# Four stages of a Perceiver kernel: pool waits by tile, one engine for token quantizing, first products before the norm, a narrower band

## The chip, the cores and the metric

The kernel runs on one core of a Trainium2 chip. A core has TensorE (PE in the profile, with its weight loads as PEld), VectorE (DVE), ScalarE (ACT), GpSimd (POOL) and SyncE (SP), whose queue issues the transfers. The engines run side by side and wait for each other by semaphores. The metric is the device time of one execution in microseconds. The kernel before took 2548.41 us (median of 3 runs, 2545.22 to 2550.57).

## The reference

A Perceiver with four layers is applied to 2 x 256 latents of 256 features. Each layer is a cross attention to a context of 2 x 4096 tokens, a self attention and a feed-forward block; each block adds its output to the stream, and the stream is normalized without parameters ahead of most blocks. What the change touches:

```
def _layernorm(x, axis=-1, eps=1e-05):
    m = jnp.mean(x, axis=axis, keepdims=True)
    v = jnp.var(x, axis=axis, keepdims=True)
    return (x - m) / jnp.sqrt(v + eps)
# L0_ffn: activations to 8 bits per token, weights to three values
def act_quant(x):
    scale = 127.0 / jnp.clip(jnp.max(jnp.abs(x), axis=-1, keepdims=True), 1e-05)
    return jnp.clip(jnp.round(x * scale), -128, 127) / scale
def weight_quant(w):
    scale = 1.0 / jnp.clip(jnp.mean(jnp.abs(w)), 1e-05)
    return jnp.clip(jnp.round(w * scale), -1, 1) / scale
def bit_linear(x, w):
    xq = x + jax.lax.stop_gradient(act_quant(x) - x)
    wq = w + jax.lax.stop_gradient(weight_quant(w) - w)
    return jnp.einsum('bsd,hd->bsh', xq, wq)
```

L0_ffn is bit_linear to 1024 hidden features, a convolution over three neighbouring tokens, SiLU, and bit_linear back. L1_ffn is a mixture of 16 experts of 128 hidden features, of which the gate picks two per token by sigmoid scores, and a shared expert that every token uses. L3_attn is a self attention in which a token sees the tokens at most 128 away. L3_ffn is a small two-layer transformer of its own; each of its layers ends with a feed-forward block of 682 hidden features with GELU gating, behind a layer norm with scale and offset.

## The kernel before

The stream x is held transposed, as two tiles of 128 features by 512 tokens (d = 0, 1). Products are in fp32, a product of 128x128 by 128x512 being two PE instructions. The function perceiver runs eleven blocks in order: l0_xattn, l0_attn, l0_ffn_and_l1_xattn, l1_attn, l1_ffn, l2_xattn, l2_attn, l2_ffn, l3_xattn, l3_attn, l3_ffn.

*The norm.* center (L221) makes the mean by products with a constant matrix, subtracts it on DVE (L232) and, with gamma given, also multiplies by it; measure (L239) squares on ACT (L233), sums by 16 small products (var), and takes root and reciprocal per token (L249, L250, the tile rstd); widen and widened spread rstd over the partitions by products (rstd_ps) and a copy on ACT (L269). layernorm (L272) does all of it and multiplies (L281, L283, L287); norm is layernorm of x.

*Order.* Where a block does not say otherwise, the framework's scheduler orders the instructions of each engine by its own model, with the program's order as priority; `nc.any` leaves the engine of a copy to it. The context attentions, L1_attn and L3_attn are written under manual_schedule of PE, DVE and ACT, whose instructions then run in the program's order. L0_ffn has only PE by program.

*Pools.* Tiles in SBUF come from pools that open and close like a stack, so a block's pool lies on the memory of an earlier block's pools. By default the first tile of a new pool waits until the earlier pools on its memory are released whole; with reuse_waits="tile" each tile waits only for the earlier tiles that it overlaps. The pools of PSUM banks and of temporaries (banks and stage, L86 and L97) wait by tile already; the blocks' pools don't.

*L0_attn and L0_ffn.* l0_attn ends with quantizing the weights of the block after it (quantize_weights, L542): w1 on DVE, w2 on POOL, with scratch tiles quant from L0_attn's work pool. l0_ffn (L1236) turns the normed stream to tokens (to_tokens, tok_ps, into hn), quantizes each token's row (quantize_tokens, L528: a maximum, four small operations on the scale, then quantize, L517, with its five steps L522 to L526), turns it back (from_tokens, L568, feat_ps, into hq), multiplies by w1 (proj), applies the convolution and SiLU (hid), and does the same for the hidden features, one tile of 128 tokens after the other (by_token, hid_tok, tok, hidq), ending with w2 (l0f_out). The rounding is `round(t) = (t * scale + MAGIC) - MAGIC`, and L525 and L526 add the rounding difference to the value as the reference does. In by_token, L525 is given to POOL:

```
net.quantize_tokens(work, tok, tok, 1, nc.gpsimd)
```

Between its steps l0_ffn runs pieces of a generator (run(between, 1)): the first three key projections of layer 1's context attention (begin, L800; k_ps, k_dense). That attention's tiles are made ahead of l0_ffn (ContextAttention, L780), and its 14 key tiles are filled with ones on POOL (L792) before rows of keys and masks are copied into them by transfers.

*L1_ffn* (L1492) norms x, multiplies the normed h by the gate's weights (gate_ps), and then goes through the shared expert (e = -1) and the 16 experts: two products into a bank pair (expert), SiLU, times the second half, times the token's share, and down (moe_acc). The routing (value, top, one, weight, wT) runs on DVE meanwhile.

*L3_attn* is SmallAttention (L1320) with a window: 8 units of batch and head group. both (L1404) makes the scores of a unit, once with queries on the partitions (for the maxima) and once with keys there; before the scores of each bank it adds the band mask, a bf16 product with the identity over all 512 columns (L1410). The mask's tile is made on POOL (mask_tile, L1861) and cast on DVE (L1881).

*L3_ffn* (L1895): in the feed-forward part of each of the two layers, layernorm gives h2, and six groups m of hidden features follow (ffn_ps, GELU, hid), then ffn_out.

## Time and profile before

The profile is of one execution.

| | |
|---|---|
| profiled execution | 2544.49 us, its span 2542.8 |
| PE busy | 2326.5 us, 91% of the span |
| DVE, ACT, POOL busy | 1544.8, 1083.0, 352.1 us |
| mean granted PE clock | 0.957 |
| L0_xattn | 0 to 704 us |
| L0_attn | 704 to 847 |
| L0_ffn | 847 to 948 |
| L1_xattn | 948 to 1630 |
| L1_attn | 1630 to 1718 |
| L1_ffn | 1718 to 1830 |
| L2_xattn, L2_attn, L2_ffn | 1830 to 1965, to 2086, to 2112 |
| L3_xattn, L3_attn, L3_ffn | 2112 to 2167, to 2271, to 2542 |

How to read the lines: the chain of waits goes back from the last instruction, at each step to what released it; its lines give start, duration, engine, tile and line of code. A timeline gives what ran in a stretch, in order, whether it is on the chain or not. A line on stretches gives the length, then each engine's busy time with its count of instructions, then the PE clock granted (1.00 is full), the DMA engines' share and GB/s.

### The profile page before, as it was taken

What the parts mean: (1) busy time and instruction counts of PE and PEld (TensorE: products, weight loads), DVE (VectorE), ACT (ScalarE), POOL (GpSimd) and SP (SyncE); (2) the same over time, 40 slices, a digit from 0 to 9 for tenths busy, and PEclk for the clock granted to TensorE, in tenths of its full rate; (3) what the DMA queues carried; (4) which work ended last, traced back from release to release, by engine and by line L of the source; (5) the groups of instructions that cost most, each with busy time, mean ns of one, the idle gap of its engine ahead of it and who ended that gap; (6) DMA issues with size and microseconds to landing.
All of it is one profiled execution on the core that took longest, in us unless ns stands there. A gap on an engine that the chain in (4) does not pass through costs nothing.

```text
span 2542.8 us, 42543 instructions
## 1 busy us (share of the span) xinstructions
PE 2326.5 (91%) x17014; PEld 1237.4 (49%) x17014; DVE 1544.8 (61%) x2702; ACT 1083.0 (43%) x1898; POOL 352.1 (14%) x523
## 2 busy tenths in 40 slices
PE   7999999999998579999999999989999986889998
PEld 3454545544544354544454544554448443445453
DVE  5878887778546467887878878343332354335252
ACT  2456555565616133555555566431131352223141
POOL 3000010000034612000010000000020131003030
PEclk9999999999999789999999999988999997998988
DMA  5432222231010133222322220202222100000100
GB/s 194 141 97 85 89 89 89 72 109 43 10 56 16 48 108 108 93 93 91 101 93 86 75 78 26 82 14 62 87 89 90 42 18 14 34 21 12 57 12 21
DMA packets 97797, 174.40 MB, mean 69 GB/s; under 512 B 15120, under 2 KB 63888, under 8 KB 96704
## 3 DMA queue, kind: packets, MB, share of 16 engines
q1 hardware_dynamic: 97600, 171.68, 21.0%
q8 instruction: 135, 2.21, 0.4%
q14 instruction: 62, 0.51, 0.1%
HBM read 154.25 MB, written 0.59 MB: 61 GB/s over the span
## 4 chain that ended last, share of the span: by engine, by line
PE 80%; DVE 10%; ACT 5%; issue 2%; POOL 1%; DMA 1%; SPq 0%; ACTq 0%; DVEq 0%; POOLq 0%
PE s L1098 11%; PE s L1122 11%; PE attn_acc L1146 9%; PE v_ps L180 6%; PE proj L180 5%; PE k_ps L1019 4%; DVE mx L1106 3%; PE f_ps L180 3%; PE expert L180 2%; PE kc_sum L180 2%; PE s L180 2%; PE c_acc L1684 2%; PE ffn_ps L180 2%; PE s L1420 2%; PE o L411 1%
## 5 line engine op out<-in xcount | busy, mean ns | idle before, releaser
L1106 DVE TENSOR_REDUCE mx<-s 128x2 f32<-128x1024 f32 x512 | 603.2, 1221 | 219.1 <-PE s L1098 216.3
L1132 ACT ACTIVATE p<-s 128x1024 f32<-128x1024 f32 x512 | 496.1, 1021 | 253.0 <-PE s L1122 250.9
L1122 PE MATMUL s<-xa_q,xa_k 32*128 32x256 f32 x4096 | 341.3, 402 | 26.0 <-DVE mx L1106 23.0
L1098 PE MATMUL s<-xa_k,xa_q 32*128 32x512 f32 x2048 | 337.5, 641 | 6.2 <-issue 2.8
L1122 PEld LDWEIGHTS s<-xa_q,xa_k 32*128 32x128 f32 x4096 | 212.0, 184 | 167.4 <-issue 92.6
L1146 PE MATMUL attn_acc<-p,xv 128*32 128x256 f32 x4096 | 275.3, 385 | 0.7 <-ACT p L1132 0.7
L657 DVE TENSOR_TENSOR ge<-fy 128x960 bf16<-128x960 f32 (+14 forms) x240 | 169.6, 707 | 6.5
L1098 PEld LDWEIGHTS s<-xa_k,xa_q 32*128 32x128 f32 x2048 | 111.4, 183 | 123.1 <-issue 62.5
L1146 PEld LDWEIGHTS attn_acc<-p,xv 128*32 128x32 f32 x4096 | 107.2, 109 | 130.8 <-issue 83.6
L611 POOL TENSOR_TENSOR fy<-fy,low 128x256 f32<-128x256 f32 x64 | 46.4, 726 | 875.5 <-ACT fy L610 875.2
L659 DVE TENSOR_TENSOR rank<-rank,ge 128x960 bf16<-128x960 bf16 (+14 forms) x240 | 104.2, 434 | 6.0
L661 DVE TENSOR_TENSOR rank<-rank,ge 128x960 bf16<-128x960 bf16 (+14 forms) x240 | 100.9, 420 | 2.6
L387 POOL TENSOR_SCALAR p<-p,r 128x128 f32<-128x128 f32 (+1 forms) x192 | 83.1, 446 | 138.4 <-DVE r L383 79.0
L1066 ACT COPY xv<-v_ps 128x512 f32<-128x512 f32 x64 | 37.6, 588 | 135.7 <-PE v_ps L180 125.8
L368 ACT ACTIVATE p<-p,top 128x256 f32<-128x256 f32 (+1 forms) x128 | 57.1, 447 | 41.5 <-DVE top L356 37.2
L180 PE MATMUL f_ps<-f_wk,f_ctx 128*128 128x256 f32 x256 | 68.9, 400 | 0.0
L233 ACT ACTIVATE sq<-xc 128x512 f32<-128x512 f32 x24 | 14.7, 630 | 126.0 <-DVE xc L232 126.0
L1019 PE MATMUL k_ps<-ctx_k,w_L0x_wq 128*64 128x512 f32 x256 | 65.5, 607 | 2.4 <-DMA ctx_k<-in_ctxT 1.9
L180 PE MATMUL v_ps<-w_L0x_wv,ctx_v 128*128 128x256 f32 x256 | 65.6, 400 | 0.8 <-ACT k_dense L1032 0.8
L1684 PE MATMUL c_acc<-pT,ctx_n 128*128 128x256 f32 x256 | 62.2, 388 | 4.2 <-ACT pT L1657 3.0
L180 PEld LDWEIGHTS f_ps<-f_wk,f_ctx 128*128 128x128 f32 x256 | 44.4, 189 | 42.7 <-issue 27.3
L180 PE MATMUL kc_sum<-f_tok,fy 128*128 128x257 f32 x256 | 64.2, 393 | 0.0
(460 smaller groups left out, 3380.0 us busy)
## 6 DMA issues: line engine op xcount, KB each, us to landing
ctx_k<-in_ctxT SPq DMA_DIRECT2D x128, 512.0 KB
ctx_v<-in_ctxT SPq DMA_DIRECT2D x64, 256.0 KB
xa_k<-k_dense SPq DMA_DIRECT2D x512, 32.0 KB
f_ctx<-in_ctxT SPq DMA_DIRECT2D x32, 256.0 KB
f_tok<-in_ctx SPq DMA_DIRECT2D x16, 512.0 KB
ctxT<-in_ctxT SPq DMA_DIRECT2D x16, 512.0 KB
ctx_n<-in_ctx SPq DMA_DIRECT2D x16, 512.0 KB
xa_k<-key_masks SPq DMA_DIRECT2D x128, 8.0 KB
```

The costliest lines, as they stand in the source:

```text
L180: self.nc.tensor.matmul(out, lhsT=lhsT, rhs=rhs, start=i == 0, stop=i == len(pairs) - 1)
L387: nc.gpsimd.tensor_scalar(p[:, j, :nk], p[:, j, :nk], r[:, j : j + 1], 1.0, ALU.mult, ALU.mult)
L657: nc.vector.tensor_tensor(ge[:, :, :n], w[:, :, :n], w[:, :, P - n :], ALU.is_ge)
L659: nc.vector.tensor_tensor(rank[:, :, P - n :], rank[:, :, P - n :], ge[:, :, :n], ALU.add)
L661: nc.vector.tensor_tensor(rank[:, :, :n], rank[:, :, :n], ge[:, :, :n], ALU.subtract)
L1019: nc.tensor.matmul(ps[i * HR : (i + 1) * HR, :], lhsT=self.wk[:, d, c * HR : (c + 1) * HR], rhs=ctx[:, d, :], start=d == 0, stop=d == ND - 1,)
L1098: nc.tensor.matmul(pairs[i // 2][:, i % 2, :], lhsT=self.q[u][rows, qt * P : (qt + 1) * P], rhs=k[rows, :], start=True, stop=True,)
L1106: nc.vector.tensor_reduce(mx[:, qt, 2 * i : 2 * i + 2, kc], sc, AX.X, ALU.max)
L1122: nc.tensor.matmul(pairs[i // 2][:, i % 2, kk * S : (kk + 1) * S], lhsT=k[rows, at], rhs=self.q[u][rows, :], start=True, stop=True,)
L1132: nc.scalar.activation(p, sc, AF.Exp, scale=DH**-0.5)
L1146: nc.tensor.matmul(self.acc[i * HP : (i + 1) * HP, :S], lhsT=v[:, 2 * k2 + kk, at : at + HP], rhs=ps[i // 2][:, i % 2, kk * S : (kk + 1) * S],
L1684: nc.tensor.matmul(accs[m], lhsT=of[:, (k + i) % (KC // P), m * P : (m + 1) * P], rhs=pT[:, i, :], start=k + i == 0, stop=k + i == KT - 1,)
```

## The change

It has six parts. (1) All pools of the blocks are opened with reuse_waits="tile". (2) quantize runs all its steps on one engine, with four scratch tiles in place of two, and returns its scratch, which holds the rounding difference; in by_token the difference is subtracted on DVE and no longer added there: from_tokens accumulates two products with the identity, of the value and of the difference, where it had one transpose. (3) The 14 key tiles of layer 1 are filled on ACT from a tile of ones in begin, and run(between, 1) is called once more in l0_ffn to run that piece. (4) L1_ffn: the gate's and the shared expert's products take the centred stream; the gate's result is multiplied by rstd per token, the shared expert's two by the widened rstd, and h is made by two multiplications. (5) L3_ffn: the first two of six groups take the centred (and scaled) stream, are multiplied by the widened rstd, and get the offset's contribution through a bias made by small products. (6) In the function both of SmallAttention, the mask's product comes after the scores and covers columns 128 to 383 of 512 alone.

```diff
@@ -446,7 +446,7 @@
-        with tc.tile_pool(name="xa", bufs=1) as big, tc.tile_pool(name="xa_ctx", bufs=2) as cpool:
+        with tc.tile_pool(name="xa", bufs=1, reuse_waits="tile") as big, tc.tile_pool(name="xa_ctx", bufs=2, reuse_waits="tile") as cpool:
...
@@ -514,18 +514,20 @@
-    def quantize(self, work, out, src, scale, inverse, low, high, first, second, third):
+    def quantize(self, work, out, src, scale, inverse, low, high, engine):
...
-        t = work.tile([P, 1024], F32, tag="quant", name="quant", bufs=2)[:, :n]
-        first.tensor_scalar(t, src, scale, MAGIC, ALU.mult, ALU.add)
-        first.tensor_scalar(t, t, MAGIC, low, ALU.subtract, ALU.max)
-        first.tensor_scalar(t, t, high, inverse, ALU.min, ALU.mult)
-        second.tensor_tensor(t, t, src, ALU.subtract)
-        third.tensor_tensor(out, t, src, ALU.add)
-    def quantize_tokens(self, work, out, src, rows, between=None):
+        t = work.tile([P, 1024], F32, tag="quant", name="quant", bufs=4)[:, :n]
+        engine.tensor_scalar(t, src, scale, MAGIC, ALU.mult, ALU.add)
+        engine.tensor_scalar(t, t, MAGIC, low, ALU.subtract, ALU.max)
+        engine.tensor_scalar(t, t, high, inverse, ALU.min, ALU.mult)
+        engine.tensor_tensor(t, t, src, ALU.subtract)
+        if out is not None:
+            engine.tensor_tensor(out, t, src, ALU.add)
+        return t
+    def quantize_tokens(self, work, out, src, rows):
@@ -535,9 +537,12 @@
         nc.vector.reciprocal(inverse, scale)
+        more = []
         for r in range(rows):
             of = scale[:, r : r + 1], inverse[:, r : r + 1]
-            self.quantize(work, out[:, r, :], src[:, r, :], *of, -128.0, 127.0, nc.vector, between or nc.vector, nc.vector)
+            to = None if out is None else out[:, r, :]
+            more.append(self.quantize(work, to, src[:, r, :], *of, -128.0, 127.0, nc.vector))
+        return more
@@ -565,13 +570,18 @@
-    def from_tokens(self, outs, src, n):
+    def from_tokens(self, outs, src, n, more=None):
...
             for i in range(k):
-                self.nc.tensor.transpose(ps[:, i * P : (i + 1) * P], src[:, (m + i) * P : (m + i + 1) * P], self.ident)
+                at, to = slice((m + i) * P, (m + i + 1) * P), ps[:, i * P : (i + 1) * P]
+                if more is None:
+                    self.nc.tensor.transpose(to, src[:, at], self.ident)
+                else:
+                    self.matmuls(to, [(of[:, at], self.ident) for of in (src, more)])
             self.copy(outs(m, k), ps[:, : k * P].rearrange("p (k t) -> p k t", k=k))
@@ -788,8 +798,9 @@
         self.key_tiles = [tile([P, KC], f"k{i}") for i in range(self.KEY_TILES)]
-        for t in self.key_tiles:
-            self.nc.gpsimd.memset(t, 1.0)
+        if layer == 0:
+            for t in self.key_tiles:
+                self.nc.gpsimd.memset(t, 1.0)
         self.begun, self.beginning = 0, iter(())
@@ -800,6 +811,10 @@
         self.begun = n
+        if self.layer > 0:
+            for t in self.key_tiles:
+                self.nc.scalar.copy(t, self.net.ones[:, 0:1].to_broadcast([P, KC]))
+            yield
         for j in range(n):
...
@@ -1239,11 +1254,12 @@
...
         h = net.norm(x)
...
         net.quantize_tokens(work, hn, hn, NT)
+        run(between, 1)
@@ -1274,15 +1290,15 @@
             nc.scalar.copy(tok[:, 0, :], sc.rearrange("p a b -> p (a b)"))
-            net.quantize_tokens(work, tok, tok, 1, nc.gpsimd)
-            toks.append(tok)
+            toks.append((tok[:, 0, :], *net.quantize_tokens(work, None, tok, 1)))
...
-            net.from_tokens(lambda m, k: hidq[:, m : m + k, at], toks[t][:, 0, :], NCH)
+            tok, more = toks[t]
+            net.from_tokens(lambda m, k: hidq[:, m : m + k, at], tok, NCH, more)
...
@@ -1404,16 +1421,9 @@
         nc = self.nc
         pairs = [self.net.sc(name) for _ in range(2)]
-        for i in range(NG if self.mask is not None else 0):
-            nc.tensor.matmul(
-                pairs[i // 2][:, i % 2, :],
-                lhsT=self.net.ident16,
-                rhs=self.mask.rearrange("p q k -> p (q k)"),
-                start=True,
-                stop=False,
-            )
         for half in range(2):
@@ -1421,9 +1431,17 @@
                     rhs=columns_of[rows, :],
-                    start=self.mask is None,
-                    stop=self.mask is None or half == 1,
+                    start=self.mask is None or half == 0,
+                    stop=self.mask is None,
                 )
+        for i in range(NG if self.mask is not None else 0):
+            nc.tensor.matmul(
+                pairs[i // 2][:, i % 2, P : P + S],
+                lhsT=self.net.ident16,
+                rhs=self.mask.rearrange("p q k -> p (q k)")[:, P : P + S],
+                start=False,
+                stop=True,
+            )
         return pairs
@@ -1496,34 +1514,54 @@
     nc.gpsimd.iota(number, pattern=[[1, E]], base=0, channel_multiplier=0, allow_small_or_imprecise_dtypes=True)
-    h = net.norm(x)
-    hc = [h[:, d, :] for d in range(ND)]
...
+    norm = net.center(net.halves(x))
...
         tile3 = lambda name: big.tile([P, NT, E], F32, name=name, tag=name)
...
         for t in range(NT):
-            net.matmuls(ps[:, t * E : (t + 1) * E], [(c[:, t * P : (t + 1) * P], gw[:, d, :]) for d, c in enumerate(hc)])
-        nc.vector.tensor_tensor(
-            value,
-            ps[:, : NT * E].rearrange("p (t e) -> p t e", t=NT),
-            gb.unsqueeze(1).to_broadcast([P, NT, E]),
-            ALU.add,
-        )
+            net.matmuls(
+                ps[:, t * E : (t + 1) * E], [(c[:, t * P : (t + 1) * P], gw[:, d, :]) for d, c in enumerate(norm.chunks)]
+            )
+        def hidden(wg, wu, of):
+            sc = net.sc("expert")
+            for n, w in enumerate((wg, wu)):
+                net.matmuls(sc[:, n, :], [(w[:, d, :], c) for d, c in enumerate(of)])
+            return sc
+        shared = hidden(sg, su, norm.chunks)
+        net.measure(norm)
+        for t in range(NT):
+            nc.vector.scalar_tensor_tensor(
+                value[:, t, :], ps[:, t * E : (t + 1) * E], norm.rstd[:, t : t + 1], gb, ALU.mult, ALU.add
+            )
         nc.scalar.activation(value, value, AF.Sigmoid)
+        factor = net.widened(norm.rstd)
+        a = work.tile([P, T], F32, tag="a", name="a", bufs=3)
+        first = work.tile([P, T], F32, tag="shared", name="shared", bufs=1)
+        nc.vector.tensor_tensor(a, shared[:, 0, :], factor, ALU.mult)
+        nc.vector.tensor_tensor(first, shared[:, 1, :], factor, ALU.mult)
+        nc.scalar.activation(a, a, AF.Silu)
+        nc.vector.tensor_tensor(first, first, a, ALU.mult)
+        h = big.tile([P, ND, T], F32, name="h", tag="h")
+        for d in range(ND):
+            nc.vector.tensor_tensor(h[:, d, :], norm.chunks[d], factor, ALU.mult)
+        hc = net.halves(h)
...
@@ -1556,19 +1594,15 @@
             if e < 0:
-                wg, wu, wd = sg, su, sd
-            elif e % 2 == 0:
-                pair = net.load(*(f"L1f_e{w}{e + i}" for i in range(2) for w in "gud"))
-                wg, wu, wd = pair[:3]
+                wd, a = sd, first
             else:
-                wg, wu, wd = pair[3:]
-            sc = net.sc("expert")
-            for n, w in enumerate((wg, wu)):
-                net.matmuls(sc[:, n, :], [(w[:, d, :], c) for d, c in enumerate(hc)])
-            a = work.tile([P, T], F32, tag="a", name="a", bufs=3)
-            nc.scalar.activation(a, sc[:, 0, :], AF.Silu)
-            nc.vector.tensor_tensor(a, a, sc[:, 1, :], ALU.mult)
-            if e >= 0:
+                if e % 2 == 0:
+                    pair = net.load(*(f"L1f_e{w}{e + i}" for i in range(2) for w in "gud"))
+                wg, wu, wd = pair[e % 2 * 3 : e % 2 * 3 + 3]
+                sc = hidden(wg, wu, hc)
+                a = work.tile([P, T], F32, tag="a", name="a", bufs=3)
+                nc.scalar.activation(a, sc[:, 0, :], AF.Silu)
+                nc.vector.tensor_tensor(a, a, sc[:, 1, :], ALU.mult)
                 share = net.mm("share")
...
@@ -1987,21 +2021,47 @@
-            h = net.layernorm([y[:, 0, :], shifted(net, work, y, 1, "shift_b")], "h2", gamma=lg, beta=lb)
-            hc = [h[:, d, :] for d in range(ND)]
+            norm = net.center([y[:, 0, :], shifted(net, work, y, 1, "shift_b")], gamma=lg)
             w2 = net.load(n("w2"))
             hid = big.tile([P, NHC, T], F32, name="hid", tag="hid")
-            for m in range(NHC):
+            def hidden(m, of):
                 k = min(P, HID - m * P)
-                at = slice(m * P, m * P + k)
                 sc = net.sc("ffn_ps")
                 for i, w in enumerate((w1a, w1g)):
-                    net.matmuls(sc[:k, i, :], [(w[:, d, at], c) for d, c in enumerate(hc)])
-                g = work.tile([P, T], F32, tag="gelu", name="gelu")
-                nc.scalar.activation(g[:k], sc[:k, 1, :], AF.Gelu, bias=b1[:k, 1, m : m + 1])
-                nc.vector.scalar_tensor_tensor(
-                    hid[:k, m, :], sc[:k, 0, :], b1[:k, 0, m : m + 1], g[:k], ALU.add, ALU.mult
-                )
+                    net.matmuls(sc[:k, i, :], [(w[:, d, m * P : m * P + k], c) for d, c in enumerate(of)])
+                return k, sc[:k, 0, :], sc[:k, 1, :]
+            def gated(m, k, a, g, bias):
+                t = work.tile([P, T], F32, tag="gelu", name="gelu")
+                nc.scalar.activation(t[:k], g, AF.Gelu, bias=bias[:k, 1, m : m + 1])
+                nc.vector.scalar_tensor_tensor(hid[:k, m, :], a, bias[:k, 0, m : m + 1], t[:k], ALU.add, ALU.mult)
+            made = [hidden(m, norm.chunks) for m in range(2)]
+            ps = net.mm("beta_ps")
+            for i, w in enumerate((w1a, w1g)):
+                for m in range(2):
+                    at = 2 * i + m
+                    net.matmuls(ps[:, at : at + 1], [(w[:, d, m * P : (m + 1) * P], lb[:, d : d + 1]) for d in range(ND)])
+            bias = big.tile([P, 2, 2], F32, name="bias", tag="bias")
+            nc.vector.tensor_tensor(bias, ps[:, :4].rearrange("p (i m) -> p i m", i=2), b1[:, :, :2], ALU.add)
+            net.measure(norm)
+            wide = net.widened(norm.rstd)
+            h = big.tile([P, ND, T], F32, name="h2", tag="h2")
+            for m, (k, a, g) in enumerate(made):
+                parts = [work.tile([P, T], F32, tag=f"by_token{i}", name=f"by_token{i}") for i in range(2)]
+                for of, part in ((g, parts[1]), (a, parts[0])):
+                    nc.vector.tensor_tensor(part, of, wide, ALU.mult)
+                if m == 0:
+                    for d in range(ND):
+                        nc.vector.tensor_tensor(h[:, d, :], norm.chunks[d], wide, ALU.mult)
+                        nc.vector.tensor_scalar_add(h[:, d, :], h[:, d, :], lb[:, d : d + 1])
+                gated(m, k, *parts, bias)
+            hc = net.halves(h)
+            for m in range(2, NHC):
+                gated(m, *hidden(m, hc), b1)
             new = net.new_x(big)
...
                 ps = net.mm("ffn_out")
```

## The prediction

> **What bounds the kernel now.** I read the page from its top down (engines, chain), then the chain of waits stage by stage for each place the diff touches, then the timeline around those places, then the stretches with their clock.
>
> ```profile
> PE 2326.5 (91%) x17014; PEld 1237.4 (49%) x17014; DVE 1544.8 (61%) x2702; ACT 1083.0 (43%) x1898; POOL 352.1 (14%) x523
> ...
> PE 80%; DVE 10%; ACT 5%; issue 2%; POOL 1%; DMA 1%; SPq 0%; ACTq 0%; DVEq 0%; POOLq 0%
> ```
>
> TensorE is busy 91% of the span and 80% of the chain. The two context attentions (0–704 and 948–1630 us) make up 54%, at clock 1.00, and the diff leaves their ordered loops alone. So the change can act only in the stages between, where the chain leaves PE. The first is the start of L0_ffn, in the chain of waits:
>
> ```profile
> 853.56 7.40 POOL quant L524 x2
> 860.96 4.60 POOL quant L525 x2
> ...
> 867.82 2.35 POOL w_L0f_w L526
> 870.19 0.70 DVE hn L219
> ...
> 870.99 1.23 DVE scale L533
> ...
> 872.24 4.78 DVE scale L534
> ```
>
> The copies into hn need tok_ps, which is complete at 859.07, and they wait until 870.19. What they wait for is GpSimd's quantizing of w2, whose scratch lies in a pool that the new pool replaces. Then a 128x4 operation (L534), 0.15 us elsewhere, takes 4.76; the timeline shows what runs beside it:
>
> ```profile
> 870.38 6.60 POOL L792 MEMSET xa_k<- 128x512 f32 x14
> ```
>
> It ends when these 14 fills end (877.0). Next the token stage of the same block, in the chain:
>
> ```profile
> 920.34 2.59 DVE quant L522
> ...
> 936.62 6.69 PE l0f_out L180 x32
> ...
> 944.42 3.84 PE l0f_out L180 x32
> ```
>
> Here DVE sets the pace (L522 takes 2.7 beside GpSimd's L525 and 0.74 alone), and one group of 32 products runs at half clock, 6.69 for 3.84. Last, one unit of L3_attn and the waist of the first L3_ffn layer, in the chain:
>
> ```profile
> 2228.38 0.59 PE sums L180 x4
> 2229.26 0.44 PE top_ps L1449 x2
> 2229.69 0.86 PE s L1410 x4
> 2230.56 1.08 PE s L1420 x16
> 2231.63 1.00 PE attn_acc L1467 x16
> 2232.63 0.97 PE s L1410 x4
> ...
> 2367.72 1.74 PE var L180 x14
> ...
> 2370.10 2.06 PE rstd_ps L180 x8
> ...
> 2372.18 1.41 DVE h L283 x2
> ...
> 2374.04 23.76 PE ffn_ps L180 x48
> ```
>
> The mask products (L1410) lie on PE's path, twice per unit of 7.58 us. In L3_ffn PE works little from 2365.69 (end of the mean) to 2374.04, and then starts 48 products at half clock. The stretches say where the clock is low:
>
> ```profile
> 853.90:888.00 34.10, 9.78 (x28) 6.09 (x29) 14.48 (x29) 1.71 (x4) 23.08 (x22) 0.50 0.11 36
> ...
> 1724.30:1737.90 13.60, 12.54 (x33) 8.11 (x34) 4.51 (x18) 2.84 (x4) 0.00 (x0) 0.50 0.00 1
> ...
> 2369.40:2379.60 10.20, 7.64 (x16) 4.24 (x16) 2.38 (x5) 1.55 (x2) 0.00 (x0) 0.50 0.01 2
> ```
>
> **The change part by part.** All sums are against the profiled execution, 2544.49 us (span 2542.8); the median of the runs, 2548.41, lies 3.9 above it.
>
> *Program start.* The fill of xa_top at 9.28 waits for the mask's transfer; key loads stand behind it on SP's queue and land at 14.96, where PE waits with k_ps. With a wait per tile the fill can go earlier. SP still issues in its old order, so I take 1.5 us; bounds 0 and 5 (nearly all of the 5.87 us transfer hidden).
>
> *L0_ffn's start.* hn overlaps oT and v of L0_attn, free at about 852, so by tile its copies start at about 859 and the reduce (1.23) ends at about 862. GpSimd's L525 and L526 of w2 then run back to back to 870.2. The nearest row, L534 held for 4.76 until the whole run of fills was over, says that DVE's small operation waits for the end of that run too: 870.2 in place of 877.0, a gain of 6.8. The 14 fills leave GpSimd for ScalarE: 14 x 0.59 (its 128x512 copy) = 8.3 us. ScalarE is idle 853.6–870.2 and is wanted next at about 873 (hq's copies came 3.8 after L535), so they hide; taken up only after 870.2, about 5.5 of them would stand before hq. SP's 14 key-mask loads only wait for these fills, and their readers come some 25 us later. I take 6.5; bounds 1 (those 5.5 show) and 16 (DVE gets between GpSimd's instructions).
>
> The Trainium skill, "SBUF — State Buffer", section "Who interferes with whom", says the loser is blocked until the other engine's instruction has finished. The row shows L534 blocked over about nine 0.525 us fills, so the run ended it, not one instruction. By the rule L534 would start at GpSimd's next boundary, about 863.3, and the whole sum would come out some 7 us lower.
>
> *Token stage.* Four times 2.35 of GpSimd's L525 goes, and DVE gets a 1.13 subtraction but loses the 1.13 addition (L526) and the 2 us of blocking: per tile 1.23 + 0.9 + 0.65 + 0.60 + 0.73 + 1.13 = 5.2 in place of 6.7. In exchange from_tokens issues 32 PE instructions per tile where it had 8 of 0.13: at 0.12 (l0f_out: 3.84/32) that is 3.84 in place of 1.06. So PE becomes the bound: 4 x (3.84 + 3.84) + 1.94 of k_ps = 32.7, from the first tile ready, 908.0 + 5.5 + 0.3 = 913.8, to 946.5, against 948.26. I take 2 us; bounds: a gain of 3 (the first tile isn't delayed by the next tile's reduce, 1.13), and a loss of 5 (two windows of half clock as at 915.3 and 935.8, each 6.8 us long and costing 3.4).
>
> *L1_ffn.* Before: mean ends 1720.27, first hidden product of an expert done at 1741.49. After: xc 0.7, gate at full clock 1.7, shared 8 x 0.43 = 3.44, var 1.74, rstd 0.5, rstd_ps 1.0, wide copy 0.6, then on DVE a, first and h, 4 x 0.69 = 2.8 with h's second half overlapped, then expert 0's 8 x 0.43 = 3.44: about 1735.9, 5.6 earlier. PE stands idle some 3 us before h. If that drops the clock, 3.44 doubles; a sigmoid table load of 1.28 ahead of the wide copy comes out of it as well. Cover for the routing (L1548's wT at 1744.06) is thinner: with experts 5.4 us earlier, wT could be late by 1 or 2. I take 4; bounds 2 and 6.5.
>
> *L3_ffn, twice.* From the mean's end to ffn_out, 32.1 now (2365.69–2397.80). After: centring with gamma 1.7, 16 products 6.9, beta 1.0, var 1.7, rstd 0.5, rstd_ps 0.95, copy 0.65, two parts 1.38, h 0.64 + 0.41 and 0.3 for its second half, 32 products 13.8 = 29.9, plus 0.3 of handovers: 1.9 less. PE idles 3.4 before h; at half clock for 6.8 us after it the layer loses 3.4, a net loss of 1.5. In the row above, half clock began after gaps of no more than 2 us, so I do not exclude it and take 1 us per layer, 2 in all; bounds −3 and +4 in all.
>
> The Trainium skill, "TensorE: Matmul & The Clock Gate", section "HAM oscillation — how this bites in real kernels", warns of PE gaps above about 3.4 us. The trace shows half clock after shorter ones. By the rule the new 3.4 us gap sits on the edge, and one lost window of about 3.4 us at half would cost 1.7 a layer and leave almost no gain.
>
> *L3_attn.* Its start: GpSimd's fills and affine selects for band_f end at 2170.5, and DVE's cast and xc stand behind them (2170.88), while the mean is done by 2169.5. By tile they go earlier: 1.5 us; bounds 0 and 3. Per unit, 8 mask products of 0.215 become 8 of about 0.107 (half the columns): −0.95 from 7.58. L1_attn's unit without mask takes 6.12; with 0.86 of mask 6.6 to 7.0. So 0.6 to 0.95 for each of five full units, and about 0.2 for each of the other groups, whose first masks already ran while DVE was reducing and now follow the scores. I take 4; bounds 2 and 6.
>
> Elsewhere (L0_attn, L1_attn, L2_xattn, L2_attn, L2_ffn) no wait for a pool stands on the chain, so waiting by tile is worth nothing there, give or take 3 for a different order of instructions.
>
> Sum: 1.5 + 6.5 + 2 + 4 + 2 + 1.5 + 4 = 21.5 us, so 2544.49 − 21.5 = 2523.0; against the median it would be 2526.9. I say 2524.
>
> **The rivals.**
>
> *PE idle and half clock eat the reordered parts.* For it: half clock follows today's short gaps in exactly these places, and the token stage has 11 us more PE work. Against it: the gaps are not longer in sum. Then the token stage loses 4, L1_ffn gains 2, L3_ffn loses 3, and the rest stands (1.5 + 6.5 + 1.5 + 4): 8.5 gained, 2536.
>
> *GpSimd gives DVE the port between instructions.* For it: at 965.98 L829 waited through one fill (1.31 in place of 0.41) with ten more to come. Against it: L534. L0_ffn's start gives 16 and not 6.5, which alone is 2513, and the parts that DVE leads gain with it: 2508.
>
> *Slower: early transfers get in front of the context's loads.* With waits by tile, loads and fills of the next block leave SP's queue as soon as single tiles are free, and SP issues in order: what waits there holds the ctx_k loads behind it. The chain of L0_xattn has one such stall already, 8.77 us on ctx_k at 67.56. Three more of that size in the two context attentions or L2_xattn (26.3) undo the sum of 21.5; from the fourth on (35.1) it decides: 2558. Against it: the DMA engines are at 0.3 of their time, and the attention's own order of loads is unchanged.
>
> *The change hardly acts:* hn overlaps the scratch that GpSimd uses or the copies are queued late, and only the bounds' low ends come: 2543 to 2550.
>
> **How the numbers follow.** Forecast case 0.57 (2513 to 2532); half clock 0.20 (2536); port 0.11 (2508); hardly acts 0.06; slower 0.06. A measurement of this kernel tells a change from none at about 0.2%, 5 us: 2543.3 to 2553.5 is the same. Faster is 0.57 + 0.20 + 0.11 = 0.88; same 0.06 (the case that hardly acts); slower 0.06. Best ends of all bounds together give about 2500, worst ends about 2550. For 8 in 10, leaving the slower case out: 2503 to 2546.
>
> **What would show it.** Right: hn's copies at about 859 and L535 near 870; no GpSimd work in the token stage, and 32-instruction feat_ps groups on the chain there; L1410 groups at half their time after the scores; gate_ps and expert ahead of var in L1_ffn, ffn_ps x16 ahead of var in L3_ffn. Wrong: hn still waiting for L526; half clock in the token stage or before h; longer DMA pieces in the chain of the context attentions.

## The result, and the profile after

The changed kernel takes 2542.59 us (median of 20 runs, 2535.51 to 2552.07) against 2547.39 (20 runs) for the kernel before. The ratio is 0.9984, 95% interval 0.9974 to 0.9993: about 4 us faster, where 21.5 were forecast. The time lies inside the range I gave, but the gain is a fifth of the one I worked out, and it is less than the 5 us (0.2%) below which I called two kernels the same.

The profiled execution of the changed kernel took 2547.81 us, 5.2 above its median, while the one of before was 2.9 below its own. So the two traces differ by +3.3 us (spans 2546.1 and 2542.8) where the medians differ by −4.8. Lengths of stages, from the first product of one block's mean to that of the next (L3_ffn in three pieces: its attention, the first feed-forward part with the second attention, the second feed-forward part), with the time at half clock in them:

| stage | before, us | half clock | after, us | half clock | forecast |
|---|---|---|---|---|---|
| L0_xattn (with the program's start) | 704.5 | 6.8 | 706.9 | 13.7 | −1.5 |
| L0_attn | 143.0 | 13.7 | 143.9 | 17.1 | 0 |
| L0_ffn | 100.5 | 47.8 | 92.4 | 30.7 | −8.5 |
| L1_xattn | 681.9 | 3.4 | 682.4 | 3.4 | 0 |
| L1_attn | 88.1 | 17.1 | 89.8 | 20.5 | 0 |
| L1_ffn | 111.3 | 13.7 | 111.0 | 13.7 | −4 |
| L2_xattn, L2_attn, L2_ffn | 283.3 | 20.4 | 280.3 | 17.0 | 0 |
| L3_xattn | 54.8 | 23.9 | 57.1 | 34.1 | 0 |
| L3_attn | 103.1 | 6.8 | 105.9 | 27.3 | −5.5 |
| L3_ffn, three pieces | 272.2 | 64.2 | 276.4 | 60.4 | −2 |

L0_ffn did what the forecast said. L3_attn, which should have lost 5.5 us, is 2.8 longer; L1_ffn stayed; L3_ffn grew. The page of the changed kernel, its engines and its chain:

```profile
PE 2346.3 (92%) x17142; PEld 1255.4 (49%) x17142; DVE 1544.8 (61%) x2719; ACT 1093.1 (43%) x1917; POOL 334.3 (13%) x505
...
PE 81%; DVE 9%; ACT 5%; issue 2%; POOL 1%; DMA 1%; SPq 0%; ACTq 0%; DVEq 0%; POOLq 0%
```

PE is busy 19.8 us more. At the start of L0_ffn, DVE's timeline (start, length, then what the engine had waited for):

```profile
861.89 0.69 DVE L219 COPY hn<-tok_ps 128x512 f32<-128x512 f32 x1 [1.00 <-PE tok_ps L568]
863.36 1.22 DVE L535 TENSOR_REDUCE scale<-hn 128x4 f32<-128x1024 f32 x1 [0.78 <-ACT hn L219]
864.61 1.86 DVE L536 TENSOR_SCALAR scale<-scale 128x4 f32<-128x4 f32 x1
866.50 0.18 DVE L537 RECIPROCAL scale<-scale 128x4 f32<-128x4 f32 x1
866.72 2.05 DVE L538 TENSOR_SCALAR scale<-scale 128x4 f32<-128x4 f32 x1
...
868.90 2.29 DVE L522 TENSOR_SCALAR quant<-hn,scale 128x256 f32<-128x256 f32 x1
873.48 0.40 DVE L522 TENSOR_SCALAR quant<-hn,scale 128x256 f32<-128x256 f32 x1 [2.29 <-POOL w_L0f_w L527]
```

hn waits for its transposes alone, as forecast. L536, L538 and L522 take about 2 us where 0.2 to 0.4 would do, beside GpSimd's L525 and L527, and a later L522 waits for the end of L527, because its scratch tile lies on one of w2's. The token stage, from the chain:

```profile
910.79 5.22 PE feat_ps L180 x30
916.01 3.68 PE l0f_out L180 x32
919.69 3.57 PE feat_ps L180 x32
923.27 3.62 PE l0f_out L180 x32
```

PE now goes from one group to the next without a wait. In L3_attn the chain shows the first units and then one of the steady units:

```profile
2200.84 2.02 PE s L1430 x16
2202.87 0.97 PE s L1438 x4
2203.83 2.97 PE s L1430 x16
...
2212.83 2.97 PE s L1430 x16
...
2229.61 0.59 PE sums L180 x4
...
2230.92 1.08 PE s L1430 x16
2232.00 0.54 PE s L1438 x4
...
2236.60 0.59 PE sums L180 x4
```

A steady unit takes 6.99 us, from one group of sums to the next (7.58 before). But in the first units a group of 16 scores takes 2 to 3 us for 1.08. And the first layer's feed-forward part in L3_ffn:

```profile
2363.61 0.86 PE mean L180 x2
2364.47 1.87 PE beta_ps L180 x16
2366.34 0.98 PE mean L180 x2
...
2369.13 7.08 PE ffn_ps L180 x16
2376.21 1.47 PE var L180 x14
...
2383.05 15.94 PE ffn_ps L180 x32
```

The products of the offset run between the two halves of the mean, and the 14 var products behind the 16 early ones. L1_ffn has the same order, 8 early products of the shared expert between the gate's and then var; the products of expert 0 wait for h until 1732.12:

```profile
1718.26 0.40 PE gate_ps L180 x2
1718.66 0.95 PE expert L180 x2
1719.61 1.47 PE gate_ps L180 x14
1721.08 4.37 PE expert L180 x6
1725.44 1.69 PE var L180 x16
...
1732.12 2.08 PE expert L180 x2
```

Stretches of the changed kernel at half clock (length, busy time of each engine, clock granted):

```profile
1728.00:1738.20 10.20, 7.60 (x15) 3.70 (x14) 8.50 (x36) 3.48 (x5) 0.52 (x1) 0.50 0.00 1
2199.00:2219.50 20.50, 18.87 (x103) 10.94 (x104) 7.01 (x8) 5.16 (x5) 0.00 (x0) 0.50 0.00 1
```

In the second one PE is busy 18.87 of 20.5 us, and still at half clock for 20 us on end. That is new in this block, which had 6.8 us at half clock in all before.

### The profile page after: what moved, and what is told of

Same layout as the page of the kernel before. It is cut to its first block, busy times and chain, and to the rows that moved or that the text cites. A ratio compares the mean times of both kernels' runs of the same rounds, so it can differ in the third digit from the quotient of the medians.

```text
span 2546.1 us, 42824 instructions
## 1 busy us (share of the span) xinstructions
PE 2346.3 (92%) x17142; PEld 1255.4 (49%) x17142; DVE 1544.8 (61%) x2719; ACT 1093.1 (43%) x1917; POOL 334.3 (13%) x505
## 4 chain that ended last, share of the span: by engine, by line
PE 81%; DVE 9%; ACT 5%; issue 2%; POOL 1%; DMA 1%; SPq 0%; ACTq 0%; DVEq 0%; POOLq 0%
PE s L1137 11%; PE s L1113 11%; PE attn_acc L1161 9%; PE v_ps L180 6%; PE proj L180 6%; PE k_ps L1034 5%; DVE mx L1121 3%; PE f_ps L180 2%; PE kc_sum L180 2%; PE expert L180 2%; PE s L180 2%; PE c_acc L1718 2%; PE ffn_ps L180 2%; PE s L1430 2%; PE o L411 1%
## 5 line engine op out<-in xcount | busy, mean ns | idle before, releaser
L1161 PE MATMUL attn_acc<-p,xv 128*32 128x256 f32 x4096 | 276.4, 386 | 0.7 <-ACT p L1147 0.7
L1113 PEld LDWEIGHTS s<-xa_k,xa_q 32*128 32x128 f32 x2048 | 111.3, 183 | 124.7 <-issue 60.1
L368 ACT ACTIVATE p<-p,top 128x256 f32<-128x256 f32 (+1 forms) x128 | 57.1, 447 | 65.5 <-DVE top L356 63.0
L180 PE MATMUL expert<-h,w_L1f_eg 128*128 128x512 f32 x128 | 61.8, 604 | 2.6 <-DVE h L1552 2.6
```

Source lines behind the costliest of these rows:

```text
L180: self.nc.tensor.matmul(out, lhsT=lhsT, rhs=rhs, start=i == 0, stop=i == len(pairs) - 1)
L1113: nc.tensor.matmul(pairs[i // 2][:, i % 2, :], lhsT=self.q[u][rows, qt * P : (qt + 1) * P], rhs=k[rows, :], start=True, stop=True,)
L1161: nc.tensor.matmul(self.acc[i * HP : (i + 1) * HP, :S], lhsT=v[:, 2 * k2 + kk, at : at + HP], rhs=ps[i // 2][:, i % 2, kk * S : (kk + 1) * S],
```

## The experiments

Theory A was: L0_ffn's gain is real; the mask products that L3_attn lost had kept PE's clock up; L3_ffn's reordering loses by itself. Its rival B: one unlucky profile. (Later theories and rivals have the letters C to G; each is given where it is tested.) Three kinds of kernels follow: parts alone and parts undone, repairs of the order, and PE's clock by itself. The kernel before was run beside each on the same chip; ratios are to it.

**The pools alone.** All `tile_pool(...)` of the blocks get the argument, nothing else:

```diff
-        with tc.tile_pool(name="xa", bufs=1) as big, tc.tile_pool(name="xa_ctx", bufs=2) as cpool:
+        with tc.tile_pool(name="xa", bufs=1, reuse_waits="tile") as big, tc.tile_pool(name="xa_ctx", bufs=2, reuse_waits="tile") as cpool:
```

> The kernel before with one part of the change alone: all block pools wait by tile. Theory A (the scratch of GpSimd's quantizing was what hn waited for, and the rest of L0_ffn's gain is the new quantizing): hn is copied near 862 as in the changed kernel, but the 14 fills stay on GpSimd behind w2 and keep holding DVE's small operations, so L0_ffn takes 96 to 99 us (100.5 before, 92.4 after), the other stages are unchanged at full clock, and the kernel is 2 to 4 us faster than before. Rival B (the pools carry all of it): L0_ffn takes 92 to 94 us and the kernel is 6 to 8 us faster.

Measured: 2550.98 us, ratio 1.0011 (0.9998 to 1.0024); L0_ffn 99.06 us. The stage is at the upper end of theory A, the whole is not there: the pools by themselves bring no time. DVE's timeline of this kernel shows why the early hn is worth only 1.5 us without the rest:

```profile
859.24 1.22 DVE L533 TENSOR_REDUCE scale<-hn 128x4 f32<-128x1024 f32 x1
860.50 0.23 DVE L534 TENSOR_SCALAR scale<-scale 128x4 f32<-128x4 f32 x1
...
867.76 9.28 DVE L522 TENSOR_SCALAR quant<-hn,scale 128x256 f32<-128x256 f32 x1 [2.31 <-POOL w_L0f_w L526]
```

L522 is held until 876.9, when the 14 fills (870.24, 6.65 us) are over. The wait for the pool goes, and the wait behind GpSimd's fills takes its place.

**The pools with the new quantizing and the fills on ScalarE.** The three other blocks as before:

```diff
-            net.quantize_tokens(work, tok, tok, 1, nc.gpsimd)
-            toks.append(tok)
+            toks.append((tok[:, 0, :], *net.quantize_tokens(work, None, tok, 1)))
...
+        if self.layer > 0:
+            for t in self.key_tiles:
+                self.nc.scalar.copy(t, self.net.ones[:, 0:1].to_broadcast([P, KC]))
+            yield
```

> The kernel before with the pools by tile, the new quantizing, the products in from_tokens and the fills on ScalarE; L1_ffn, L3_attn and L3_ffn as before. Theory A: L0_ffn 92 to 93 us, the rest as before, the whole 8 us faster than before (2539.5), that is 3 us faster than the whole change, because the other three parts together lose. Rival B: the other three parts gain on average and the profiled execution of the whole change was unlucky in its clock; then this kernel is 3 us or more slower than the whole change.

Measured: 2541.03 us, ratio 0.9980 (0.9965 to 0.9994); L0_ffn 90.92 us. So this part is worth about 5 us (1.5 to 9 by the interval), the whole of what the change brings. Of its three pieces only the pools were also run alone. The three others together bring nothing; whether they lose something (theory A said 3 us) is within the interval.

**Without the part in L3_ffn.** The feed-forward part of its layers as in the kernel before:

```diff
-            norm = net.center([y[:, 0, :], shifted(net, work, y, 1, "shift_b")], gamma=lg)
...
-            made = [hidden(m, norm.chunks) for m in range(2)]
+            h = net.layernorm([y[:, 0, :], shifted(net, work, y, 1, "shift_b")], "h2", gamma=lg, beta=lb)
```

> The whole change without its part in L3_ffn. Theory A (in L3_ffn the small products of the offset run ahead of the mean's second half, the variance stands behind 16 products, and the gap before h is longer): the last two stages fall back from 182.7 to about 179.6 us, at full clock from 171.7 to 165, and the kernel is 4 to 7 us faster than the whole change. Rival B (half clock by chance in one profile): within 2 us of the whole change.

Measured: 2542.09 us, ratio 0.9978 (0.9965 to 0.9990). In the trace the last two pieces take 179.6 us, as theory A said, but the medians are equal within the intervals: no effect of the part in L3_ffn on the time is seen. Rival B holds here for the time, but not for its reason: these two pieces have 33.1 us at half clock in the changed kernel and 40.3 in this one, so it is not more half clock that makes them 3 us longer there. Why the trace shows a loss and the medians don't is not settled. The granted clocks of all executions give a hint: 0.9563 on average in the 20 of the changed kernel and 0.9541 in these 12. Twice what is missing from 1, times the span, is an estimate of the time at half clock: some 222 and 233 us. So the part may cost work and save half clock elsewhere.

**Without the part in L3_attn.** Wide mask ahead of the scores again:

```diff
+                pairs[i // 2][:, i % 2, :],
-                pairs[i // 2][:, i % 2, P : P + S],
```

> The whole change without its part in L3_attn, whose mask products are again ahead of the scores and 512 columns wide. Theory A (the wide mask products kept PE at full clock while DVE worked in the first units; without them it drops to half for about 20 us): L3_attn 101 to 104 us with at most 10 us at half clock, against 105.9 with 27.3 at half in the changed kernel, and the whole time within 2 us of it. Rival B (the phase of the clock's windows is chance): L3_attn usually takes 96 to 98 us in the changed kernel, and this one is 4 to 6 us slower than the whole change.

Measured: 2546.64 us, ratio 0.9993 (0.9980 to 1.0007). L3_attn takes 104.56 us with 6.8 at half clock. The clock part of theory A is there, and not by chance: the four traces with the narrow mask in all units (the changed kernel, the run before this one and the next two) have 27.3, 27.3, 27.3 and 23.9 us at half clock in this block, the five with the wide one 6.8 to 13.7. In the whole time the narrow mask is ahead by some 2 us (0.9984 for 0.9993), at the edge of theory A's bound, but the intervals overlap, and in the traces its block is 1.3 us longer (105.9 for 104.56). So it is not shown that the steady units gain more than the first units lose.

**The norm measured first.** Theory C, for the other two parts: var comes behind the early products on PE, as the lines of the changed kernel show, so these don't fill the wait for rstd, they stand in front of it.

```diff
         value = tile3("value")
+        net.measure(norm)
         ps = net.mm("gate_ps")
...
         shared = hidden(sg, su, norm.chunks)
-        net.measure(norm)
...
+            net.measure(norm)
             made = [hidden(m, norm.chunks) for m in range(2)]
```

> The whole change, but in L1_ffn and L3_ffn the norm is measured (var, root, reciprocal) ahead of the early products in the program, so that the scheduler lets PE take var among them and not behind them. Theory C (the early products gained nothing because var stands behind them in PE's queue, so that the whole wait for rstd comes after them at its old length): var ends some 4 us sooner after the mean, L1_ffn takes 107 to 109 us (111.0 in the changed kernel), the last two stages together 3 to 5 us less than 182.7, and the kernel is 4 to 7 us faster than the whole change. Rival D (half clock takes whatever these places gain): L1_ffn 110.5 to 111.5, and within 2 us of the whole change.

Measured: 2544.47 us, ratio 0.9978 (0.9965 to 0.9992); L1_ffn 112.21 us. The gain that theory C forecast did not come. The block is no shorter, and 13.7 us of it are at half clock again, as rival D had it. But the edit did not make the order that theory C asks for:

```profile
1713.90 2.78 PE var L180 x14
1716.67 3.62 PE expert L180 x4
1720.30 1.72 PE rstd_ps L180 x8
```

var ends 8.2 us after the mean for 9.6 in the changed kernel, 1.5 sooner and not 4, and then the products that spread rstd stand behind the last four early ones. So what the early products would give with var and rstd_ps both ahead of them is not shown.

**The offset's products at the head of the layer**, on top of that:

```diff
             scales = net.vec(n("scales"))
+            ps = net.mm("beta_ps")
...
-            ps = net.mm("beta_ps")
```

> As the run before, and the offset's small products (beta_ps) of L3_ffn are made at the head of each layer, not between the two halves of the mean. Theory C: the mean of the feed-forward part ends 1.3 us sooner in each layer, and 1 us of PE work is added elsewhere in the layer: 1 to 3 us faster than the run with the measure moved alone. Rival D: within 1 us of it.

Measured: 2551.10 us, ratio 1.0016 (1.0002 to 1.0030): some 10 us slower than the run before it by the ratios, 7 by the medians, against theory and rival. The mean does end sooner, but half clock then begins at 2364.5 and 14 early products take 8.61 us for 6.12. The piece with the first feed-forward part takes 134.1 us with 34.1 at half clock, for 125.2 with 17.1: a reordering that shortens a wait was worse by the clock.

**The wide mask in the first three units only:**

```diff
+        for i in range(NG if wide else 0):
+            nc.tensor.matmul(
+                pairs[i // 2][:, i % 2, :],
...
-        for i, sc in enumerate(self.both("s1", self.q[u], self.keys(u))):
+        for i, sc in enumerate(self.both("s1", self.q[u], self.keys(u), u < 3)):
```

> The whole change, but the first three units of L3_attn keep the wide mask ahead of the scores, and only the later units have the narrow one behind them. Theory A (the wide products kept PE's clock up in the units that DVE paces): at most 10 us of L3_attn at half clock (27.3 in the changed kernel), L3_attn 99 to 102 us in place of 105.9, the kernel 3 to 5 us faster than the whole change. Rival B (chance): half clock and time of L3_attn vary as before, 96 to 106, and the kernel is within 2 us of the whole change. Rival E (the mask behind the scores delays the reductions, and the clock has no part in it): L3_attn 102 with as much half clock as now.

Measured: 2536.92 us, ratio 0.9957 (0.9940 to 0.9974). L3_attn 101.79 us with 6.8 at half clock. The first units in one stretch, from the first score product to the first steady unit, in the changed kernel and then in this one:

```profile
2196.10:2223.40 27.30, 24.24 (x162) 14.43 (x162) 11.19 (x13) 6.26 (x7) 0.00 (x0) 0.62 0.09 33
```

```profile
2189.40:2213.00 23.60, 16.90 (x162) 8.94 (x164) 11.54 (x15) 6.26 (x8) 0.00 (x0) 1.00 0.12 44
```

More work on PE, 7 us less PE time, 3.7 us less in all, at clock 1.00. Theory A stands; rivals B and E fall. Two limits: the wide mask also stands ahead of the scores here, and a wide mask behind them or a narrow one ahead was not run; and of the some 7 us by which this kernel is ahead of the changed one, L3_attn has 4.1 in the traces, while L1_ffn, in which nothing was edited, is 2.5 shorter with 6.9 less at half clock.

**All three together.**

> All three together: measure first, the offset's products at the head of the layer, wide masks in the first three units of L3_attn. Theories A and C: 9 to 14 us faster than the whole change, about 2530. Rivals: 2540, within 3 us of the whole change.

Measured: 2548.90 us, ratio 0.9991 (0.9974 to 1.0009). Neither theory's number: the gain of the wide mask (L3_attn 101.81) is undone by the two orders of the runs before, above all in the piece with the first feed-forward part, 134.5 us with 34.1 at half clock. Three of the twelve executions took 2533 to 2539 us, the other nine 2544 to 2555.

**What sets the clock.** At this point I laid all ten traces on the grid on which their clock changes, stretches of 3.413 us, and counted for each what PE streamed: for every PE instruction of a product its columns, twice for fp32, times the share of the 128 rows and of the 128 columns of the array that it uses. By this count 512 fp32 columns are 1024, and take 0.43 us at clock 1.00, so a full stretch has about 8192. A small product (one column, as in var) counts next to nothing, however long PE is busy with it. The count of one stretch tells the clock of the next. In all 14 traces of this case, the four of the next runs included, 10355 stretches:

| full columns in a stretch | stretches | the next one at half clock |
|---|---|---|
| under 2500 | 638 | 99% |
| 2500 to 2900 | 177 | 92% |
| 2900 to 3100 | 119 | 66% |
| 3100 to 3300 | 107 | 5% |
| 3300 to 3700 | 212 | none |
| over 3700 | 9102 | none |

Ends of products are modelled in the records, and some records may be missing, so the rows near the mark are blurred. With one threshold at 3050 the count agrees with the clock in 99.5%. At half clock a stretch can hold about 4096, so PE must be three quarters full to get out. L3_attn's first units stand on that edge. In the changed kernel the stretches from 2199 on hold 2210, 2861, 2573, 2496, 2474 and 3277 at half clock, and after the last of them the clock is full again. With the wide mask in front (the run with the first three units) they hold 4300, 4716, 2824, 4982 and 4903 at full; the third is one of the exceptions. The kernel before fell to half clock at the same place, behind a stretch of 2184, but its wide masks put 3303 into the one stretch at half, and it came out. The kernel before has a second witness: L1_attn is the same function without a mask, and there the first units run at half clock, 17.1 us of the block, with groups of 16 scores at twice the 1.08 us that they take later:

```profile
1658.55 2.09 PE s L1420 x16
...
1664.65 2.03 PE s L1420 x16
...
1670.68 2.02 PE s L1420 x16
```

The next four runs test this as theory F.

**Unread products in the waits of L1_ffn and L3_ffn**, on top of the wide mask in the first units:

```diff
     def widened(self, rstd, name="wide", spare=0):
         wide = self.temp.tile([P, T], F32, tag=name, name=name, bufs=1)
         self.nc.scalar.copy(wide, self.widen(rstd))
+        for _ in range(spare):
+            self.widen(rstd)
```

> The whole change with the wide mask in L3_attn's first three units, and in L1_ffn and L3_ffn the products that spread rstd are made three times, twice into banks that nobody reads (16 PE instructions of 0.11 us, 4096 streamed columns), while PE waits for h. Theory F, from all ten traces so far: a 3.41 us stretch in which PE streams fewer than about 3050 full columns is followed by one at half clock, otherwise by one at full, so the gains of the reordered places were lost to half clock because those places are nearly empty of columns. Then half clock after the waist goes: L1_ffn 107 to 108 us, the last two stages 176 to 180 us, the kernel 3 to 6 us faster than with the wide mask alone. Rival G (the wait itself is the loss, whatever PE streams in it): L1_ffn 108.5 to 111, the last two stages 181 to 185, and the same time as with the wide mask alone or 1 us more.

Measured: 2535.15 us, ratio 0.9951 (0.9934 to 0.9968); L1_ffn 106.67 with 3.4 us at half clock, the last two pieces 181.6. L1_ffn is as theory F said, 4.4 us less than in the changed kernel, but 1.8 less than with the wide mask alone (108.5, with 6.8 at half clock), which is the run to compare with. The last two pieces are in rival G's range. Where the unread products stand they do act: the 32 products behind them take 14.13 us in each layer, for 16.87 and 16.00 with the wide mask alone. But the 16 early products take 9.83 and 9.78 us, since the stretches ahead of them stay under the mark (2076 and 2078 columns). The whole differs from the wide mask alone by less than the intervals tell.

**The wide mask first, without the part in L3_ffn.** The edits of two earlier runs together.

> The whole change with the wide mask in L3_attn's first three units and without the part in L3_ffn. If the two effects add: L3_attn 102, the last two stages 179.6, the kernel 2 to 4 us faster than with the wide mask alone, about 0.994 to 0.995 of the kernel before. If the part in L3_ffn costs only by the chance of its clock: the same as with the wide mask alone, 0.9957.

Measured: 2537.60 us, ratio 0.9957 (0.9937 to 0.9977), the same as with that part (2536.92, 0.9957), as far as the intervals tell. The mean clocks differ in the same sense as above, 0.9582 without the part and 0.9605 with it.

**L1_ffn and L3_ffn as before, and unread products in every plain norm:**

```diff
         self.matmuls(mean, [(self.share, x) for x in chunks])
+        for _ in range(spare):
+            self.matmuls(self.mm("spare"), [(self.share, x) for x in chunks])
...
         wide = self.widen(n.rstd)
+        for _ in range(1):
+            self.widen(n.rstd)
```

> Pools, L0_ffn and the band as changed (wide mask in the first three units), L1_ffn and L3_ffn as before the change, and in each plain norm (L0_ffn, L1_ffn, L2_ffn, L3_xattn or L3_ffn's first, the two feed-forward parts of L3_ffn) the products of the mean and those that spread rstd are made once more, unread, in PE's idle time. Theory F: less half clock at each of these, L1_ffn 107 to 109, the last two stages 173 to 178, the kernel 5 to 10 us faster than the run without the part in L3_ffn. Rival G: same as that run, or 1 to 3 us slower by the added products.

Measured: 2521.21 us, ratio 0.9899 (0.9871 to 0.9928), the fastest of all and faster than both kernels of the case. The mean granted clock of its six executions is 0.967, for 0.954 in the kernel before beside it. L1_ffn takes 105.28 us with 1.3 at half clock, the last two pieces 175.2. One profile line for the 24 us around L1_ffn's norm in this run, where the kernel before had 13.6 us at 0.50:

```profile
1701.00:1725.00 24.00, 23.23 (x89) 13.03 (x88) 10.53 (x33) 6.25 (x9) 0.00 (x0) 1.00 0.11 33
```

**The kernel before, and only the unread products.** The same edit on the kernel before.

> The kernel before with nothing but the unread second products of mean and rstd in its plain norms. Theory F: half clock falls by 20 to 40 us in all, the kernel is 6 to 12 us faster than before (ratio 0.995 to 0.998). Rival G: half clock and time unchanged, or slower by up to 5 us.

Measured: 2532.14 us, ratio 0.9933 (0.9907 to 0.9959): 17 us faster, without a single useful instruction changed, and four times what the change brought. Theory F stands, with a larger size than expected; rival G falls. The clock of the executions shows it: 0.958 to 0.964 granted in these six, 0.950 to 0.958 in the 23 of the kernel before beside them. The trace alone would not: it is of the slowest of the six (2544.45 us), and has 215.9 us at half clock where the kernel before had 217.7. In the six pieces with such a norm (L0_ffn, L1_ffn, L2_ffn and the three of L3_ffn) half clock fell from 135.9 to 91.0 us; in the others, where nothing was edited, it rose from 81.8 to 124.9, for which no run here gives a reason. In this execution L1_ffn is 105.52 us where it was 111.33, and the chain of L3_ffn's first feed-forward part shows the added products in the wait for shift_b:

```profile
2367.26 0.86 PE mean L180 x2
2368.12 1.05 PE spare L180 x2
2369.16 0.87 PE mean L180 x2
...
2372.06 1.74 PE var L180 x14
...
2378.21 20.99 PE ffn_ps L180 x48
```

48 products in 20.99 us, where they took 23.76.

## Why the prediction was wrong, step by step

**L0_ffn's start: right in size (6.5 taken).** From the block's first mean product to the first token's reduce it is 53.5 us for 60.4 before, 6.9 less. Of the mechanism, half was right. I had DVE wait for the end of GpSimd's whole run, because L534 had waited out nine fills. In the changed kernel it got in between: L536, L538 and L522 each waited for about one GpSimd instruction. The Trainium skill, "SBUF — State Buffer", section "Who interferes with whom", says just that, the loser waits for the whole instruction of the other, and these rows agree with it (1.86, 2.05 and 2.29 us beside instructions of 2.3). Beside fills L534 before, and L522 in the run with the pools alone (9.28 us), waited for the whole series, which is more than one instruction. The gain still stopped at 6.9, since the last wait is for a tile, not for the port: L522 at 873.48 starts when the last of GpSimd's L527 ends. So the size came out right for a reason that I had not given, which is luck.

**Token stage: right (2 taken, 1.2 measured).** From that reduce to the end it takes 38.9 us for 40.1. PE became the bound at 32 instructions per tile, as worked out. The sum had full clock there, and it came nearly so: 3.4 us at half clock for 13.6 before.

**Program start: right in kind, smaller in size (1.5 taken, 0.4 measured).** The transfer that k_ps waits for starts at 8.10 for 9.05 us, but takes 6.39 for 5.87, so k_ps starts at 14.54 for 14.96. It is lost again behind it: L0_xattn has 13.7 us at half clock for 6.8.

**L3_attn's start: wrong (1.5 taken, nothing measured).** The fill of sa_v still waits for the block before: its tile lies on memory that the projection reads. POOL's timeline after:

```profile
2163.22 1.05 POOL L1351 MEMSET sa_v<- 128x1148 f32 x1 [26.52 <-PE proj L180]
```

**L3_attn's units: the step that failed most.** The steady unit was right (6.99, between my 6.6 and 7.0). The step "about 0.2 for each of the other groups, whose first masks already ran while DVE was reducing and now follow the scores" was wrong by its sign: the first units cost 3.7 us more. I counted the mask products as work to be hidden or not. They also were half of what kept PE above the clock's mark while DVE led: scores and masks of a unit stream 8192 full columns with the wide mask and 6144 with the narrow one. At half clock the unit gets longer (9.0 us for 5.8 with the wide mask at full), so its count per stretch falls further, and the state holds itself up until the steady units come. Three wide masks took the 3.7 us back. The profile before could have told me: in L1_attn, without a mask, the first units ran at half clock.

**L1_ffn (4 taken, 0.3 measured).** The sum put "gate at full clock 1.7, shared 8 x 0.43" and expert 0's products at full clock. Gate and shared took 7.18 us together for 5.14, and from 1728.0 to 1738.2 the clock was at half, the same 13.7 us in all as before. Without that assumption there is nothing to gain: the exposed chain from var over root, rstd_ps and copy to h is no shorter behind the early products (6.7 us, from 1725.44 to 1732.12) than it was ahead of them (5.7). What the place could give was the clock, 5.8 us, and unread products gave it without a reordering. I had seen the half clock and put it into the bounds (a gain of 2); it belonged in the middle, and the 0.3 measured lies below even that bound.

**L3_ffn (2 taken; 4.3 lost in the trace, and no difference in the medians without it).** I had put the offset's products (1.0 us) behind the early ones; the scheduler put them, at 1.87 us, between the halves of the mean, where they cost 1.35 us. From the mean's end to ffn_out, for which I had 30.2, the layers took 31.7 and 35.7 us (32.1 and 32.2 before). The term that failed is the products at full clock: the last 32 took 15.94 and 16.61 us for 13.8, and in the second layer the first 16 took 9.56 for 6.9, so that half clock came twice there, 17.0 us for 10.2. In the three pieces together there is less half clock than before (60.4 us for 64.2); what else makes them 4.3 longer is only in part known (the 1.35 per layer).

**The stages that don't change** add 4.7 us in the trace, with 20.5 us more at half clock (L0_xattn, L0_attn, L1_attn and L3_xattn have more, L2_attn less); "give or take 3" was too narrow. The clock's grid does not start with the program: its first boundary lies 0.1 to 3.0 us behind the program's start, elsewhere in each of the 14 traces. So the same work can fall on it in another way from one execution to the next.

**The rivals.** The first one, half clock in the reordered parts, was the right kind. I set it aside with "the gaps are not longer in sum", and left L3_attn out of it. Gaps are not what counted here: the Trainium skill, "TensorE: Matmul & The Clock Gate", section "HAM oscillation — how this bites in real kernels", warns of gaps over about 3.4 us as well, and in L3_attn half clock came with no such gap (the longest is 2.32 us) and PE 92% busy. The other section that bears on it, "What's actually happening", speaks of a free-running window of activity; the stretches of 3.41 us in these traces agree, and the counts say what activity is. The rival of the port was half right: DVE did get in between GpSimd's instructions at L0_ffn's start, but the wait for a tile left nothing of the further gain. The rival in which the change hardly acts has nearly the measured time, but not its reason: hn did come early, and what it gained was lost elsewhere. The rival of stalled context loads did not occur: DMA's share of the chain is still 1%. With the clock held by three wide masks the change is worth 11 us (0.9957), half the forecast, the chance 2.5 us in L1_ffn included.

## What to carry to other kernels

Before a change takes work off TensorE, or moves it, count what it streams per 3.4 us there: below about 37% of the array's full columns (3050 of 8192) the next stretch ran at half clock in these traces, whether the engine was idle, waited, or was busy with products of few columns or rows. In the norms between blocks, where PE waits for other engines, a product that nobody reads can be worth more than a cleverer order; here it was 17 us. Look also for a stage that already does without the work you are about to take away, as L1_attn did. And a stage time from one profile carries the luck of the clock's grid: compare medians of runs for the whole, and half-clock time beside each stage.

## What I had not expected of the hardware

- The clock of a 3.41 us stretch followed the count of full columns in the stretch before, with a mark near 3050 of 8192, in 99.5% of 10355 stretches. Rows and columns of the array count: weighted by both, 866 of 875 half-clock stretches follow one under the mark; by columns streamed alone, at the mark that suits it best, 631 do.
- Near the mark half clock can hold itself up, because a stretch at half clock holds half as many columns. In L3_attn 20.5 us in a row were at half clock with PE busy 18.87 of them.
- DVE's small operations waited for one instruction beside GpSimd's operations that read SBUF (1.86 to 2.29 us) and for a whole series beside its fills (4.76 us before, 9.28 us in the run with the pools alone, of which the fills were 6.65). There is one exception in the traces: in the kernel before, L829 at 965.98 took 1.31 us for 0.41 and got in beside the first of eleven fills in a row.
